# Cross-attention and a scanned state space on one Trainium2 core: scores and value products on quarters of the TensorE array, one shared PSUM bank fewer, and the end of the kernel as planned pieces

## The chip, the core and the metric

The kernel runs on one core of one Trainium2 chip. The metric is device time in microseconds (us) of one execution. Before the change three runs took 2513.02, 2515.10 and 2516.12 us; the median is 2515.1 us. One more execution was profiled; it took 2515.3 us, of which 2513.5 us lie between the first and the last instruction (the span).

## The reference, cut to what matters

There is one batch entry, 4096 query rows of width 512, 3202 context rows, 8 heads of width 64, and everything is float32.

```python
x = _layernorm(builder_state, g1, beta1)
base_n = _layernorm(base_state, g1, beta1)
x = residual + _mha(x, base_n, W_qkv, b_qkv, W_o, b_o)   # softmax(q k^T / 8) v, then W_o
xn = _layernorm(x, g2, beta2)
U = (xn @ W_in.T + b_in) @ Bmat                          # 4096 x 64
def step(s, u_t):
    s = jax.nn.silu(s @ A.T) + u_t
    return (s, s)
_, states = jax.lax.scan(step, 0, U)                     # 4096 steps, one after another
x = residual + states @ Cmat
mod = program_probs.mean(axis=1) @ W_prog.T + b_prog
return x + mod
```

The attention is the large part: 4096 x 3202 scores for each of 8 heads, the exponential of each, and the product of the weights with the values. The scan is sequential, but its state is forgotten quickly, so the kernel runs it in many stretches at once and checks whether the start of each stretch agrees with the end of the one before.

## The kernel before, in words

**Preparation** (the first 258 us of the profile). The context is normalized, turned and multiplied with the weights; keys and values are written to device memory (`kd`, `vd`). Small matrices of the scan are made beside it.

**The loop over steps.** The queries are cut into 8 blocks of 512 rows. A *unit* is one block, one pair of heads (`hp`, two heads of 64 make 128 partitions) and one half of the block (256 queries, `QU`). There are 64 units. A unit goes through the keys in 13 *steps*; a step takes two groups of 122 to 124 keys (`b` is 0 or 1) for both heads of the pair (`a` is 0 or 1). So there are 832 steps, and each of them does this:

- `scores` (L605, TensorE): four matmuls, one for each `b` and `a`. The 64 rows of one head contract, so each uses half of the rows of the array, and the 123 keys are its output partitions. The result `s` is [keys, a, b, 256] and fills two PSUM banks, one for each head.
- `keep` (L618, ScalarE) copies `s` to SBUF as `p`; `running` (L633, VectorE) keeps the running maximum over the steps in `top`.
- After the 13th step the maximum over keys is taken across partitions: `spread` (TensorE transposes, tile `tt`), `maximum` (VectorE), `everywhere` (TensorE, tile `mb`).
- `subtract` (L664, VectorE) and `weights` (L674, ScalarE, the exponential) work on `p` in place.
- `product` (L691, TensorE): four matmuls, one for each `b` and `a`. All 123 keys contract, and the 64 value columns of a head are half of the columns of the array. They accumulate over the 13 steps in one bank, `po`.
- `add` (L682, GpSimd) sums the weights over the steps into `acc`; this is the denominator.

The float32 matmul of one call appears in the profile as two weight loads and two matmuls, so both `scores` and `product` have 8 records of each kind in a step.

At the end of a unit, `output` (L737) copies `po` to SBUF, `both`, `turn`, `inverse`, `wide` and `back` turn the denominator into a factor, and `scale` applies it. Once in a block, the rows are projected (`outs`, L900), normalized, and turned into inputs of the scan (`inputs`, `kept`); the queries of the next block are normalized and projected beside it (`heads`, L294).

**PSUM** has 8 banks. The loop gives 4 to `s` (two buffers of two banks), 1 to `mb`, 1 to `po`, and 2 to a pool `ps_m`, from which every other piece of TensorE work takes its bank: `spread`, `turn`, `back`, the transposes of queries and rows, `heads`, `outs`, `inputs`.

**The order.** The order of the instructions on each engine is written out by hand through a planner (`Plan`, L54). Every piece has an engine, a cost, the pieces that it follows, a due time (step number times `STEP`, shifted by `SHIFT` for its sort) and the buffers that it takes and gives back. `order` (L92) lists the pieces by a simulated clock: when an engine is free, it takes the ready piece with the earliest due time whose buffers fit. For scores and products it adds 200 ns (`START`) when the kind of TensorE work changes and 65 (`AGAIN`) when it stays, and prefers runs of two of one kind (`RUN`). On the chip each engine then runs its list strictly in that order. The transfers are issued by SyncE from the same lists: `load_k` in the score pieces and `load_v` in the score or product pieces.

**The last unit and the end.** For the last unit six of the 13 partial denominators are made by TensorE with a matrix of ones (`PE_SUMS`, L708) instead of GpSimd. When the planner's pieces are through, `main_scan` (L1136) and `last_rows` (L1175) run as two Python generators that are advanced in turn. The scan makes two sweeps of 16 steps over all stretches (`sweep`, L1062): sweep a from zero, sweep b from the ends that sweep a found. A scan step is a matmul (L1072), a tanh on ScalarE (L1085) and a product on VectorE (L1086). Sweep a also issues bfloat16 matmuls on zeros (L1078). In sweep b, each step adds `states` (GpSimd), `products` (L1102, TensorE) and `outputs` (additions on VectorE, ScalarE and GpSimd, and two stores). `last_rows` takes the last 256 rows through projection, normalization and 24 short scan steps of their own (L1250). A comparison of ends and starts (`differ`) closes the kernel, and a correcting loop follows it that runs only where they differ.

## Time and profile before

| What | us |
|---|---|
| median of three runs | 2515.1 |
| the profiled execution, and its span | 2515.3, 2513.5 |
| preparation, to the first score matmul | 257.9 |
| scores of the first unit, to the first product | 257.9 to 295.7 |
| loop, first product to last score | 295.7 to 2398.4 |
| last products and denominators | to 2436.6 |
| sweep a and the last rows | 2436.6 to 2462.5 |
| sweep b with the outputs, and the short scan | 2462.5 to 2502 |
| last outputs, comparison, end | 2502 to 2513.5 |

| In 600 to 2100 us | busy us of 1500 |
|---|---|
| PE (TensorE matmul) | 1480.17 |
| POOL (GpSimd) | 1414.12 |
| DVE (VectorE) | 1391.14 |
| ACT (ScalarE) | 1289.17 |

In these 1500 us some 580 steps pass, 2.59 us each. The columns of a group row are: line, engine, operation, output and inputs, shapes, count, then busy time in us and the mean ns of one, then the idle time of the engine just before them and what ended it. PEld is the loading of weights, which runs beside the matmuls. Busy time counts an overlap once.

### The profile page before, as it was taken

Reading aid. Unit: us, or ns where it says so; the run is one execution under the profiler, and the core shown is the slowest. Engines: PE = TensorE matmul, PEld = TensorE weight load, DVE = VectorE, ACT = ScalarE, POOL = GpSimd, SP = SyncE. Lnnn points to the kernel's source line nnn. Section 1 sums busy time; section 2 is a strip of 40 time slices with the busy share of each in tenths; the row PEclk is TensorE's granted clock in tenths of the full one; section 3 lists DMA queues with packets and bytes.
Section 4 is the critical chain, followed back from the end, with each engine's and each line's share of the span. In section 5 each row is a group of like instructions: output and inputs, shape, how many; then the busy total and the mean of one; then the engine's idle time right before and its main releaser. Section 6 shows DMA issues by size and latency. Waiting matters only on the chain.

```text
span 2513.5 us, 43994 instructions
## 1 busy us (share of the span) xinstructions
PE 2418.6 (96%) x16390; PEld 1409.1 (56%) x16392; DVE 2087.6 (83%) x2242; ACT 1922.3 (76%) x2373; POOL 2066.7 (82%) x1195
## 2 busy tenths in 40 slices
PE   7999899999999999999999999999999999999987
PEld 3444555655565555655565556555565556555543
DVE  2220699999999989899999999999989899999964
ACT  2222588878987898788987898789878888888852
POOL 1110299989998999899998999899989999899963
PEclk9999999999999999999999999999999999999998
DMA  3422322112211222122211221222212221233364
GB/s 120 131 99 79 88 64 62 45 48 68 66 56 53 66 66 66 49 62 85 64 49 43 68 78 46 60 67 67 58 48 67 74 64 53 83 115 118 107 165 144
DMA packets 178035, 189.21 MB, mean 75 GB/s; under 512 B 14252, under 2 KB 151256, under 8 KB 177818
## 3 DMA queue, kind: packets, MB, share of 16 engines
q1 hardware_dynamic: 173270, 178.67, 23.7%
q10 hardware_dynamic: 4548, 7.67, 1.0%
q8 instruction: 133, 2.18, 0.4%
q14 instruction: 84, 0.69, 0.1%
HBM read 156.40 MB, written 29.89 MB: 74 GB/s over the span
## 4 chain that ended last, share of the span: by engine, by line
PE 38%; DVE 22%; POOL 17%; issue 13%; ACT 6%; DMA 2%; SPq 1%; ACTq 0%; POOLq 0%; DVEq 0%
POOL acc L682 15%; DVE top L633 12%; PE s L605 12%; PE po L691 9%; DVE p L664 6%; ACT p L618 3%; PE pv L534 3%; PE pk L560 3%; PE pq L294 3%; PE pa L900 2%; ACT p L674 2%; PE tt L641 1%; POOL both L747 1%; PE pd L753 1%; DMA cx<-in_ctx_dram 1%
## 5 line engine op out<-in xcount | busy, mean ns | idle before, releaser
L682 POOL TENSOR_TENSOR acc<-p,acc 122x1024 f32<-122x1024 f32 (+1 forms) x698 | 1653.0, 2368 | 60.7 <-ACT p L674 17.9
L664 DVE TENSOR_TENSOR p<-p,mb 123x1024 f32<-123x1024 f32 (+2 forms) x832 | 991.7, 1208 | 23.2 <-PE mb L656 23.2
L674 ACT ACTIVATE p<-p 123x1024 f32<-123x1024 f32 (+2 forms) x832 | 875.4, 1058 | 138.9 <-DVE p L664 134.2
L618 ACT COPY p<-s 123x1024 f32<-123x1024 f32 (+2 forms) x832 | 829.6, 1006 | 168.4 <-PE s L605 121.6
L605 PE MATMUL s<-q,k 64*123 64x256 f32 (+2 forms) x6656 | 911.1, 398 | 25.2 <-DVE top L633 15.0
L691 PE MATMUL po<-p,v 123*64 123x256 f32 (+2 forms) x6656 | 877.5, 390 | 6.6 <-ACT p L674 4.7
L633 DVE TENSOR_TENSOR top<-s,top 123x1024 f32<-123x1024 f32 (+1 forms) x640 | 777.3, 1215 | 11.5 <-ACT p L618 9.3
L605 PEld LDWEIGHTS s<-q,k 64*123 64x123 f32 (+2 forms) x6656 | 574.9, 182 | 337.7 <-DVE top L633 115.9
L691 PEld LDWEIGHTS po<-p,v 123*64 123x64 f32 (+2 forms) x6656 | 423.5, 136 | 357.9 <-issue 145.5
L682 POOL TENSOR_TENSOR acc<-p,p 124x1024 f32<-124x1024 f32 x64 | 152.3, 2380 | 121.2 <-DMA k<-kd 73.8
L633 DVE TENSOR_TENSOR top<-s,p 124x1024 f32<-124x1024 f32 x64 | 78.2, 1222 | 99.3 <-ACT p L618 66.3
L294 PE MATMUL pq<-xn,wq 128*128 128x256 f32 x512 | 126.7, 390 | 0.0
L243 POOL TENSOR_SCALAR ve_c<-mv_c 123x1 f32<-123x1 f32 (+2 forms) x26 | 6.1, 233 | 145.7 <-DVE mv_c L236 117.8
L900 PE MATMUL pa<-wo,o 128*128 128x512 f32 x240 | 116.9, 609 | 0.0
L504 DVE COPY ct<-tp_c 128x492 f32<-128x492 f32 (+2 forms) x13 | 8.7, 672 | 123.3 <-PE tp_c L270 123.3
L294 PEld LDWEIGHTS pq<-xn,wq 128*128 128x128 f32 x512 | 92.2, 189 | 31.6 <-issue 21.2
L568 ACT ACTIVATE ks<-pk,bias 128x492 f32<-128x492 f32 (+3 forms) x28 | 18.0, 643 | 118.6 <-PE pk L560 58.4
L534 PE MATMUL pv<-wv,ct 128*123 128x512 f32 (+2 forms) x208 | 99.0, 621 | 0.0
L560 PE MATMUL pk<-ct,wk 128*128 128x492 f32 (+3 forms) x224 | 89.1, 550 | 0.0
L747 POOL TENSOR_TENSOR both<-acc 124x512 f32<-124x512 f32 x63 | 80.8, 1283 | 3.0
L648 DVE TENSOR_REDUCE m<-tt 128x4 f32<-128x496 f32 x64 | 42.9, 671 | 42.7 <-PE tt L641 42.7
L534 PEld LDWEIGHTS pv<-wv,ct 128*123 128x123 f32 (+2 forms) x208 | 39.1, 196 | 46.0 <-issue 45.1
(196 smaller groups left out, 1486.3 us busy)
## 6 DMA issues: line engine op xcount, KB each, us to landing
k<-kd SPq DMA_DIRECT2D x324, 123.0 KB
v<-vd SPq DMA_DIRECT2D x324, 123.0 KB
k<-kd SPq DMA_DIRECT2D x108, 124.0 KB
v<-vd SPq DMA_DIRECT2D x108, 124.0 KB
xr<-in_x_dram SPq DMA_DIRECT2D x32, 256.0 KB
x1d<-xr SPq DMA_DIRECT2D x32, 256.0 KB
x<-in_x_dram SPq DMA_DIRECT2D x28, 256.0 KB
cx<-in_ctx_dram SPq DMA_DIRECT2D x18, 246.0 KB
```

What stands on the lines that cost most here:

```text
L294: nc.tensor.matmul(pq[:, half * QU : (half + 1) * QU], wq[:, i, hp * P : (hp + 1) * P], xns[half][:, i, :], start=(i == 0), stop=(i == NC ...
L534: nc.tensor.matmul(pv[:n, :H], ct[:, i, o : o + n], wv[:, i, :], start=(i == 0), stop=(i == NC - 1),)
L560: nc.tensor.matmul(pk[:, :n_g], wk[:, i, hp * P : (hp + 1) * P], ct[:, i, :n_g], start=(i == 0), stop=(i == NC - 1),)
L605: nc.tensor.matmul(s[:n, a, b, :], kts[(*w["at"][:2], c)][r, b * n : (b + 1) * n], q[r], start=True, stop=True,)
L618: nc.scalar.copy(t[:n], w["ps"][c][:n])
L633: nc.vector.tensor_tensor(w["top"][:n], s[:n], before[:n], ALU.max)
L664: nc.vector.tensor_tensor(t[:n], t[:n], w["mb"][:n].unsqueeze(2).to_broadcast([n, 2, 2, QU]), ALU.subtract,)
L674: nc.scalar.activation(t[:n], t[:n], AF.Exp)
L682: nc.gpsimd.tensor_tensor(w["acc"][:n], t[:n], before[:n], ALU.add)
L691: nc.tensor.matmul(w["po"][a * HD : (a + 1) * HD, 0, :], vts[(*w["at"][:2], c)][:n, b, a * HD : (a + 1) * HD], t[:n, a, b, :], start=(c == ...
L747: nc.gpsimd.tensor_tensor(w["both"], acc[:, :, 0, :], acc[:, :, 1, :], ALU.add)
L900: nc.tensor.matmul(v["pa"], o_t[Q, c, t // 2][:, t % 2 * P : (t % 2 + 1) * P], wo[:, c, :], start=(c == 0), stop=(c == NC - 1),)
```

## The change

Five things change.

1. `scores` makes eight matmuls in a step: the keys of a group are cut at 64, so that each matmul uses 64 rows and at most 64 columns of the array. The output goes to the upper or the lower half of the partitions of the same two banks.
2. `product` makes eight matmuls in a step: the keys that contract are cut at 64 too. The two key halves accumulate in two banks of a wider `po`. `output` copies the first, and a new VectorE operation for each unit, `join`, adds the second.
3. The second bank of `po` comes from `ps_m`, which has one bank in the loop instead of two. In the preparation a second pool `ps_n` keeps two.
4. The planner counts 10 ns for a change between scores and products and 200 after other work, runs are of one, and the table `SHIFT` is new.
5. The end of the kernel becomes pieces of the plan. Sweep a may start as soon as the last scores have left their banks, beside the last unit's products; the matmuls on zeros are gone. Sweep b starts when sweep a has ended, and the last rows start when the last unit is through. `products` is issued in two halves of 256 columns. In the last unit TensorE makes three of the partial denominators instead of six, GpSimd nine.

```diff
-    START, AGAIN = 200, 65
-    RUN = 2
-    ALONE = dict(scores=600, product=2600)
+    START, AGAIN = 200, 10
+    RUN = 1
+    ALONE = dict(scores=300, product=1300)
...
-                    cost += (self.AGAIN if same else self.START) if p["kind"] else 0
+                    cost += (self.AGAIN if last else self.START) if p["kind"] else 0
...
-    ps_m = actx.enter_context(tc.tile_pool(name="ps_m", bufs=2, space=PSUM))
+    ps_m = actx.enter_context(tc.tile_pool(name="ps_m", bufs=1, space=PSUM))
+    m_pools = [ps_m]
+
+    def m_tile(shape, name):
+        pool = m_pools.pop(0)
+        m_pools.append(pool)
+        return pool.tile(shape, F32, tag="m", name=name)
...
+    m_pools.append(prep.enter_context(tc.tile_pool(name="ps_n", bufs=1, space=PSUM)))
...
+    m_pools[:] = [ps_m]
     prep.close()
...
         for b in range(2):
-            for a in range(2):
-                r = slice(a * HD, (a + 1) * HD)
-                nc.tensor.matmul(
-                    s[:n, a, b, :],
-                    kts[(*w["at"][:2], c)][r, b * n : (b + 1) * n],
-                    q[r],
-                    start=True,
-                    stop=True,
-                )
+            for k0, k1 in ((0, HD), (HD, n)):
+                for a in range(2):
+                    r = slice(a * HD, (a + 1) * HD)
+                    nc.tensor.matmul(
+                        s[k0:k1, a, b, :],
+                        kts[(*w["at"][:2], c)][r, b * n + k0 : b * n + k1],
+                        q[r],
+                        start=True,
+                        stop=True,
+                        skip_group_check=True,
+                    )
...
-            w["po"] = ps_o.tile([P, 2, QU], F32, tag="o", name=f"po_{w['name']}")
+            w["po"] = ps_o.tile([P, 2, 2 * QU], F32, tag="o", name=f"po_{w['name']}")
         for b in range(2):
             for a in range(2):
-                nc.tensor.matmul(
-                    w["po"][a * HD : (a + 1) * HD, 0, :],
-                    vts[(*w["at"][:2], c)][:n, b, a * HD : (a + 1) * HD],
-                    t[:n, a, b, :],
-                    start=(c == 0 and b == 0),
-                    stop=(c == NDC - 1 and b == 1),
-                )
+                for k, (k0, k1) in enumerate(((0, HD), (HD, n))):
+                    nc.tensor.matmul(
+                        w["po"][a * HD : (a + 1) * HD, k, :QU],
+                        vts[(*w["at"][:2], c)][k0:k1, b, a * HD : (a + 1) * HD],
+                        t[k0:k1, a, b, :],
+                        start=(c == 0 and b == 0),
+                        stop=(c == NDC - 1 and b == 1),
+                        skip_group_check=True,
+                    )
...
+    def join(w):
+        o = o_t[w["at"]]
+        nc.vector.tensor_tensor(o, o, w["po"][:, 1, :QU], ALU.add)
...
-    PE_SUMS = range(2, NDC, 2)
+    PE_SUMS = (4, 8, 12)
+    A_PACE, B_PACE = 1500, 1900
...
-            elif fill:
-                for _ in range(fill):
-                    nc.tensor.matmul(
-                        sv["fill"], zeros[:, :P], zeros, start=True, stop=True
-                    )
...
-    def products(j, s):
+    def products(j, s, part=slice(0, H)):
         for v, n in enumerate(counts):
             r = slice(v * NS, (v + 1) * NS)
-            nc.tensor.matmul(sv["py"][j % 2][v], s[r, :], sv["c2"][r], start=True, stop=True)
+            nc.tensor.matmul(
+                sv["py"][j % 2][v][:, part], s[r, :], sv["c2"][r, part], start=True, stop=True,
+                skip_group_check=True,
+            )
...
+            plan.add(("join", i), "DVE", 400, partial(join, w), [("output", i)], d + 500, [],
+                     [("o", ("product", i, 0))])
...
+        plan.add("start", "DVE", 600, ready_scan, ["fetch"] + kept_, d + 2 * STEP, ["s", "s"])
...
+        for p in sweep("a", None, "end1", d + 3 * STEP, A_PACE, ["start"]):
+            plan.add(*p)
+
+        d += 16 * STEP
+        last_unit(plan, ws[n], n, d)
+        last_rows(plan, d)
+        for p in sweep("b", "end1", "end0", d + STEP, B_PACE, [("a", "end")]):
+            plan.add(*p)
...
+                plan.add(("products", j, part), "PE", 590, partial(products_, j, part),
+                         [("states", j), *free[j % 2]], e + 1000 + part)
...
-                s=2, m=2, b=1, o=1, p=NDC + LAG + 4, top=2, acc=2, both=1, q=6, x=3, x1=2, xn2=1,
+                s=2, m=1, b=1, o=1, p=NDC + LAG + 4, top=2, acc=2, both=1, q=6, x=3, x1=2, xn2=1,
...
-        for _ in last_rows(ws[len(units) - 1]):
-            next(scan, None)
-        for _ in scan:
-            pass
-        last_outputs("a")
-        differ(sv["sl"][:, : P : LT], sv["st"], P // LT, sv["badl"])
```

## The prediction

> **What bounds the kernel now.** I begin with the page's first two parts: busy time by engine, and the span in 40 slices.
>
> ```profile
> PE 2418.6 (96%) x16390; PEld 1409.1 (56%) x16392; DVE 2087.6 (83%) x2242; ACT 1922.3 (76%) x2373; POOL 2066.7 (82%) x1195
> ...
> PE   7999899999999999999999999999999999999987
> ...
> DVE  2220699999999989899999999999989899999964
> ACT  2222588878987898788987898789878888888852
> POOL 1110299989998999899998999899989999899963
> ```
>
> In the loop (slices 6 to 38) three engines stand at 9, so relief for one alone may buy little. The second view is the same in microseconds for a stretch of the loop, and for the end. Its columns are: length, then PE, PEld, DVE, ACT and POOL busy (instructions), the granted TensorE clock, the DMA share, GB/s.
>
> ```profile
> 600.00:2100.00 1500.00, 1480.17 (x10749) 884.04 (x10750) 1391.14 (x1400) 1289.17 (x1570) 1414.12 (x765) 1.00 0.21 62
> 2436.60:2462.50 25.90, 21.23 (x102) 11.94 (x102) 10.58 (x30) 7.07 (x22) 4.58 (x8) 1.00 0.45 116
> 2462.50:2498.00 35.50, 32.13 (x140) 15.57 (x140) 22.22 (x67) 13.02 (x45) 19.83 (x27) 0.99 0.61 205
> ```
>
> PE works 98.7% of the loop and its clock is full, so it sets the pace: 2.59 us for a step. How near the others are behind it is seen in their waits. Third view, waits on VectorE and GpSimd from 298 to 2403 us: in total, times, longest.
>
> ```profile
> POOL acc L682 <- ACT p L674: 63.9, 44, 5.6
> ...
> DVE top L633 <- ACT p L618: 66.8, 59, 2.4
> DVE m L648 <- PE tt L641: 41.9, 37, 2.0
> DVE p L664 <- PE mb L656: 17.0, 14, 1.7
> DVE s L627 <- ACT p L618: 8.8, 11, 1.7
> ```
>
> GpSimd waits 63.9 of 2105 us, 3.0%, though it is busy only 94%: the rest lies between its instructions. In the timeline five additions in a row take 12.19 us, and one takes 2.37 (row L682), so they start 12.19 less 2.37, over 4, or 2.45 us apart; 0.08 us of each is a gap that nobody ends. GpSimd without waits would need 2.59 x 0.970 = 2.51 us for a step. VectorE waits 135.9 us with a small fifth row, 6.5%, so its floor is 2.42. **The loop is bound by PE, and 0.08 us behind it stands GpSimd, which the change doesn't relieve.**
>
> Fourth view, PE's timeline (start, length from first start to last end, line, operation, count):
>
> ```profile
> 1301.29 1.99 PE L605 MATMUL s<-q,k 64*123 64x256 f32 x16
> 1303.21 1.08 PE L691 MATMUL po<-p,v 123*64 123x256 f32 x8
> ...
> 1305.81 1.13 PE L605 MATMUL s<-q,k 64*123 64x256 f32 x8
> 1306.87 1.08 PE L691 MATMUL po<-p,v 124*64 124x256 f32 x8
> 1307.89 0.44 PE L771 MATMUL rb<-ident,wide 128*128 128x128 f32 x2
> ```
>
> By the starts, scores alone hold PE 1.06 us (1305.81 to 1306.87) and products 1.02. Two score steps in a row hold it 1.92, so the second costs only 0.86. A change of kind thus costs 0.20 before scores and 0.16 before products; without one, eight matmuls in pairs take four slots of 0.216 us.
>
> **The change, part by part. Quarters.** The streamed columns stay: a step's scores become 16 matmul records instead of 8, and if four run at once instead of two they again take four slots, 0.86 us. What can go is the price of changing kind. The row cannot tell whether scores and products in quarter form count as one kind. Here the Trainium skill helps (TensorEngine Tiling (Array Packing), Key Properties): a change of tiling mode drains the array, a change of tile within a mode doesn't, and both would now be 64 x 64. So I take 0.86 for either. Had each kept its change, a step would hold 1.06 + 1.02 as now.
>
> Can it be issued so fast? Twice as many records in the same time are 16 loads and 16 matmuls in 0.86 us. The densest row that is sustained are the one-column matmuls of the preparation:
>
> ```profile
> 116.94 0.54 PEld L438 LDWEIGHTS pb<-bi,bm 128*64 128x64 f32 x8 [0.16 <-issue]
> 116.94 0.63 PE L438 MATMUL pb<-bi,bm 128*64 128x1 f32 x8
> 117.40 0.55 PEld L442 LDWEIGHTS pb<-be2s,wcr 128*64 128x64 f32 x8
> ```
>
> Eight loads with eight matmuls start in 0.46 us (116.94 to 117.40), 58 ns for a pair, on one tile, where each matmul also waits for its own load. Sixteen would be 0.92 us. A rule speaks against even that: TensorE: Matmul & The Clock Gate, Part 1, puts the sequencer at some 62 ns for each matmul when hardware decode is off, 0.99 us for sixteen. The row is under it, so it decides. Lower end 0.86 (slots), upper end 0.92; I take 0.87, since loads of different tiles overlap in L605, where a pair of tiles starts as one.
>
> A second rule speaks against it more strongly: the same page, Part 3, says a weight load overlaps a running matmul only in other rows of the array. By it each quarter slot would add a load of 0.136 us (mean of the L691 loads): 4 x 0.352 = 1.41 us, and the step below would come to 3.50. But L691 uses all rows, has eight such loads, and still holds PE 1.02 us. I keep the row.
>
> PE's other work, from the groups of the trace (busy time of L294 126.7, L900 116.9, L656 42.4, L641 40.6, L753 40.4, L948 32.6, L771 27.6 and 40.4 of L270 for queries and rows), is 467.6 us over 832 steps, 0.56 a step. About 7.5 such pieces in a unit of 13 steps (four of its own, 28 in a block of eight units) each still force a change back, 0.20, so 0.12 a step. PE after: 2 x 0.87 + 0.56 + 0.12 = 2.42 us (2.52 at the upper end). That is no longer the bound; GpSimd at 2.51 is. VectorE gets one `join` for a unit, near the 0.41 us of L779, which has the same size: 0.03 a step, 2.45. It lies in VectorE's waits; if there were none, it would cost 64 x 0.41 = 26 us.
>
> So at most GpSimd's 63.9 us can go. Three engines between 2.42 and 2.51 in strict order won't run without waits; I take half of it, **32 us** (a step of 2.55). Ends: nothing and 64.
>
> **One bank for everything else.** Its users in a unit are `tt`, `pd` and `rb`, and in a block 20 more, so 44 in 104 steps, 352 in all. PE waits with all that is behind it (scores and products, and so ScalarE, VectorE and GpSimd) when the reader of the bank before is late. PE's slack against today's pace is 2.59 - 2.42 = 0.17 us a step, 138 us in all, or 0.39 us for each user. I put the cost at nothing within the 32: the planner counts the bank as taken, and other matmuls stand between users.
>
> **First unit.** 13 score steps run with little beside them; each loses its change of kind, 0.20 us: **3 us**.
>
> **The end.** Sweep a moves beside the last unit's products, and with it 15 of the L1072 matmul pairs, tanhs and products; no transfer moves with it. From 2436.6 on, PE is busy 21.2 of 25.9 us, then 32.1 of 35.5, so the end is mostly PE work too, and moving it saves only what it idles (4.7 + 3.4, and 2.7 between 2403 and 2436.6: 10.8 us) and what is left out: the matmuls on zeros (L1078, 7.3 us) and three sums at 0.86 (2.6). Against it: 16 scan matmuls between products are changes of kind, 16 x 0.16 = 2.6. At best 10.8 + 7.3 + 2.6 - 2.6 = 18 us. In the list of the changed kernel the sweep's matmuls stand between the last unit's products, and sweep b begins before the last product, so half of the idle time should go: 18 - 5 = 13, less 3 for GpSimd's three added partial sums (7.3 us of additions that lie beside VectorE's 13 subtractions for the most part). **10 us.** Ends: -10 (each scan step waits in three queues behind pieces of 0.9 to 1.2 us) and 18.
>
> Sum: the profiled execution's span is 2513.5, its time 2515.3; 2515.3 - 32 - 3 - 10 = 2470.3. It lies 0.2 over the median of the runs shown, so **2470 us**.
>
> **The rivals.**
> *B, GpSimd holds the loop where it is.* If its waits come from unit boundaries (44 of them, all on weights, about one for a unit), a faster PE need not shorten them: the chain from last score to maximum to first weight runs through VectorE and ScalarE. For it: VectorE's waits for `tt` too. Against: that chain contains scores and transposes that queue behind PE. Only first unit and end are won: 2502. The change then doesn't do what it says in the loop.
> *C, waits vanish.* GpSimd becomes the only bound, buffers fill, and boundaries are bridged: 2515 - 64 - 3 - 18 = 2430.
> *D, slower: the single bank stalls PE.* Place: any second user of `ps_m` at the head of PE's list. It decides from 0.39 us for each of 352 users, plus what the end wins (13 / 352 = 0.04). A full VectorE operation of 1.2 us that has to pass before the reader, half of the time, is 0.6: 352 x (0.6 - 0.43) = 60, so 2575.
> *E, slower: quarters don't run four at a time at full pace.* From 0.955 us for eight (2 x 0.955 + 0.68 = 2.59) the loop is slower; at 1.08 (a slot of 0.27, one 0.055 us load exposed) a step is 2.84, 0.25 x 813 = 203 more: some 2700.
>
> **How the numbers follow.** Mine 0.45, B 0.23, C 0.13, D 0.12, E 0.07. Mine spans 2450 to 2490. The time is mine, 2470. The range leaves out D and E at the top and the lowest of C: 2422 to 2514. Faster or slower by 0.2% (5 us) is about what a measurement tells from no change. Mine, C and 0.20 of B are faster, 0.78; 0.04 is same; slower is 0.18.
>
> **What would show it.** Sixteen matmuls of L616 starting within 0.86 to 0.93 us, and a product after scores at that distance too: right on the quarters. GpSimd's waits under 40 us and PE near 94% in the loop: right on the bound. PE idle before scores, ended by a reader of `ps_m`: D. Scan steps with a distance of over 2.5 us beside the last unit: the end is dearer. Were GpSimd's additions themselves to change from 2.37 us, my floor would be wrong in either direction.

## The result, and the profile after it

The changed kernel takes 2486.5 us (median of four runs, 2485.2 to 2487.9), the kernel before it 2515.2 (median of four beside it, 2513.0 to 2516.1). The ratio is 0.989, with a 95% interval of 0.9876 to 0.990. The prediction was 2470 us with a range of 2422 to 2514: the direction and the range held, and the point was 16.5 us too low.

The profiled execution's span fell from 2513.5 to 2483.4 us, by 30.1. First come the page's busy times and slices of the changed kernel.

```profile
PE 2296.9 (92%) x29718; PEld 1355.7 (55%) x29718; DVE 2108.2 (85%) x2307; ACT 1917.3 (77%) x2373; POOL 2071.5 (83%) x1197
...
PE   7999888999999999999999999999998999999987
...
DVE  2111599999999999999999999999999999999975
ACT  2223588888987899788988988789978998888852
POOL 1111199989998999989998999899999999899984
```

TensorE has nearly twice the records and 121.7 us less busy time. VectorE and GpSimd have nearly the same work as before (VectorE 20.6 us more, with 64 `join` operations of 0.41 us in it). The span fell by only a quarter of what TensorE lost. Next, the same stretch of the loop as before, and the two parts of the end: from the last score to the last product, and from there to the end. The columns are length; busy time of PE, PEld, DVE, ACT and POOL; the granted TensorE clock, the DMA share, GB/s. First the kernel before, for the end only, then the changed one.

```profile
2398.40:2434.50 36.10, 32.19 (x212) 17.28 (x210) 23.69 (x30) 19.39 (x21) 30.36 (x15) 0.91 0.67 177
2434.50:2513.50 79.00, 59.75 (x274) 30.90 (x272) 38.03 (x117) 21.01 (x71) 25.47 (x35) 0.90 0.49 152
```

```profile
600.00:2100.00 1500.00, 1419.59 (x20232) 864.54 (x20224) 1422.35 (x1463) 1301.43 (x1588) 1431.93 (x773) 1.00 0.22 64
2373.20:2422.30 49.10, 43.35 (x398) 22.05 (x392) 31.14 (x52) 23.26 (x38) 39.94 (x20) 0.97 0.73 192
2422.30:2483.40 61.10, 44.33 (x256) 27.77 (x248) 33.05 (x99) 16.32 (x54) 24.88 (x34) 0.84 0.44 149
```

In the loop TensorE now works 94.6%, VectorE 94.8% and GpSimd 95.5% of the time: three engines stand within one per cent of each other. At the end the last unit became longer (36.1 to 49.1 us) and what follows it shorter (79.0 to 61.1), together 4.9 us less.

Placed on the time axis, the 30.1 us are: 1.5 us more until the first score (257.9 and 259.4), 0.7 less in the first unit (34.3 and 33.5 from its first score to its first subtraction), 25.9 less in the loop (2106.2 and 2080.3 from there to the last score), and 4.9 less at the end.

The waits of VectorE and GpSimd, in the changed kernel from 298 to 2370 us (in total, times, longest):

```profile
DVE m L660 <- PE tt L653: 57.6, 35, 3.9
...
POOL acc L694 <- ACT p L686: 46.7, 54, 2.8
...
ACT p L630 <- POOL acc L694: 24.4, 28, 2.2
...
DVE p L676 <- PE mb L668: 22.2, 24, 1.6
...
DVE top L645 <- ACT p L630: 8.0, 26, 0.9
```

GpSimd's waits for weights fell from 63.9 to 46.7 us, VectorE's wait for scores that are kept (L645, before L633) from 66.8 to 8.0; its wait for the transposes of the maximum (`tt`) rose from 41.9 to 57.6. Last, TensorE's timeline of the changed kernel at the place that the prediction showed (start, length from first start to last end, line, operation, count):

```profile
1301.80 1.09 PE L705 MATMUL po<-p,v 64*64 64x256 f32 x16
1302.72 1.05 PE L616 MATMUL s<-q,k 64*64 64x256 f32 x16
1303.58 1.05 PE L705 MATMUL po<-p,v 64*64 64x256 f32 x16
...
1307.62 1.93 PE L705 MATMUL po<-p,v 64*64 64x256 f32 x32
1309.35 1.07 PE L616 MATMUL s<-q,k 64*64 64x256 f32 x16
```

Scores that follow products hold TensorE 0.86 us (1302.72 to 1303.58), and two products in a row 1.73 (1307.62 to 1309.35). The counts are records, two for each matmul. So the sixteen records of a step's quarters take the time that eight records of halves took without a change of kind, and between scores and products that price is gone.

### The profile page after: what moved, and what is told of

It reads as the page before. It is cut to its first block, busy times and chain, and to the rows that moved or that the text cites. A ratio compares the mean times of both kernels' runs of the same rounds, so it can differ in the third digit from the quotient of the medians.

```text
span 2483.4 us, 70816 instructions
## 1 busy us (share of the span) xinstructions
PE 2296.9 (92%) x29718; PEld 1355.7 (55%) x29718; DVE 2108.2 (85%) x2307; ACT 1917.3 (77%) x2373; POOL 2071.5 (83%) x1197
## 3 DMA queue, kind: packets, MB, share of 16 engines
q8 instruction: 237, 3.88, 0.7%
## 4 chain that ended last, share of the span: by engine, by line
PE 44%; DVE 21%; POOL 13%; issue 10%; ACT 8%; DMA 2%; SPq 1%; ACTq 0%; POOLq 0%; DVEq 0%
PE s L616 13%; PE po L705 12%; POOL acc L694 12%; DVE top L645 12%; DVE p L676 6%; PE pq L302 5%; ACT p L630 4%; ACT p L686 3%; PE pv L543 3%; PE pk L569 3%; PE pa L902 1%; PE mb L668 1%; PE tt L653 1%; PE pd L755 1%; DMA x<-in_x_dram 1%
## 5 line engine op out<-in xcount | busy, mean ns | idle before, releaser
L694 POOL TENSOR_TENSOR acc<-p,acc 122x1024 f32<-122x1024 f32 x701 | 1660.3, 2369 | 64.1 <-ACT p L686 26.2
L616 PE MATMUL s<-q,k 64*64 64x256 f32 (+3 forms) x13312 | 884.9, 384 | 90.9 <-DVE top L645 79.9
L705 PE MATMUL po<-p,v 64*64 64x256 f32 (+3 forms) x13312 | 857.3, 379 | 26.9 <-ACT p L686 25.1
L645 DVE TENSOR_TENSOR top<-s,top 123x1024 f32<-123x1024 f32 (+1 forms) x640 | 777.4, 1215 | 11.8 <-ACT p L630 11.3
L616 PEld LDWEIGHTS s<-q,k 64*64 64x64 f32 (+3 forms) x13312 | 448.2, 130 | 428.6 <-DVE top L645 154.5
L705 PEld LDWEIGHTS po<-p,v 64*64 64x64 f32 (+3 forms) x13312 | 489.8, 133 | 268.4 <-ACT p L686 70.0
L302 PEld LDWEIGHTS pq<-xn,wq 128*128 128x128 f32 x512 | 92.2, 189 | 34.3 <-issue 23.6
L645 DVE TENSOR_TENSOR top<-s,p 124x1024 f32<-124x1024 f32 x64 | 78.0, 1219 | 37.8 <-DMA k<-kd 31.8
L902 PEld LDWEIGHTS pa<-wo,o 128*128 128x128 f32 x240 | 40.6, 189 | 51.9 <-issue 50.8
```

Of the source, the lines that this page charges most:

```text
L302: nc.tensor.matmul(pq[:, half * QU : (half + 1) * QU], wq[:, i, hp * P : (hp + 1) * P], xns[half][:, i, :], start=(i == 0), stop=(i == NC ...
L616: nc.tensor.matmul(s[k0:k1, a, b, :], kts[(*w["at"][:2], c)][r, b * n + k0 : b * n + k1], q[r], start=True, stop=True, skip_group_check=True,)
L645: nc.vector.tensor_tensor(w["top"][:n], s[:n], before[:n], ALU.max)
L694: nc.gpsimd.tensor_tensor(w["acc"][:n], t[:n], before[:n], ALU.add)
L705: nc.tensor.matmul(w["po"][a * HD : (a + 1) * HD, k, :QU], vts[(*w["at"][:2], c)][k0:k1, b, a * HD : (a + 1) * HD], t[k0:k1, a, b, :], sta ...
L902: nc.tensor.matmul(v["pa"], o_t[Q, c, t // 2][:, t % 2 * P : (t % 2 + 1) * P], wo[:, c, :], start=(c == 0), stop=(c == NC - 1),)
```

## A view that the averages hide

From the second query block to the seventh the loop repeats itself every eight units (one block), to 0.3 us. The units of such a block are unlike each other, because the projections of queries (the heads) and of outputs fall into a few of them. So I cut one block into its units, each from its first subtraction to that of the next. These are the windows of the changed kernel for the units 16 to 23.

```profile
819.20:851.66 32.46, 30.52 (x434) 17.97 (x426) 31.89 (x35) 28.42 (x35) 31.51 (x19) 1.00 0.31 88
851.66:883.16 31.50, 30.08 (x443) 18.07 (x442) 30.66 (x33) 27.72 (x37) 30.79 (x18) 1.00 0.18 55
883.16:919.60 36.44, 34.90 (x485) 21.19 (x484) 33.12 (x34) 33.98 (x47) 35.31 (x25) 1.00 0.28 86
919.60:952.38 32.78, 30.78 (x425) 17.48 (x427) 30.91 (x33) 29.54 (x41) 31.97 (x22) 1.00 0.18 59
952.38:985.35 32.97, 30.03 (x474) 18.43 (x478) 32.44 (x33) 30.23 (x38) 32.02 (x17) 1.00 0.27 72
985.35:1020.52 35.17, 35.17 (x434) 22.86 (x430) 31.21 (x33) 27.49 (x31) 34.23 (x16) 1.00 0.11 31
1020.52:1052.73 32.21, 32.17 (x498) 21.53 (x494) 30.35 (x32) 26.03 (x29) 31.02 (x15) 1.00 0.24 65
1052.73:1085.48 32.75, 27.99 (x438) 15.53 (x438) 32.34 (x33) 26.90 (x30) 26.88 (x12) 1.00 0.16 48
```

Read the largest of PE (second number), DVE (fourth) and POOL (sixth) in each line against the length. The length is that largest number plus 0 to 1.1 us, and the engine that has it changes: VectorE in the 1st, 5th and 8th unit, GpSimd in the 2nd, 3rd and 4th, TensorE in the 6th and 7th. In the 6th, which has three heads, TensorE has no idle time at all (35.17 of 35.17); in the 8th it idles 4.8 us. The second engine stands only 0.1 to 1.2 us behind the largest in the first seven. The largest number says which engine has least room, not yet which one holds the unit; e6 and e11 below show the difference. The kernel before, for the same block:

```profile
822.50:854.07 31.57, 31.09 (x219) 17.78 (x220) 30.43 (x32) 27.59 (x34) 29.96 (x18) 1.00 0.23 69
854.07:890.85 36.78, 36.35 (x266) 21.61 (x266) 32.80 (x34) 31.91 (x43) 35.82 (x22) 1.00 0.21 65
890.85:924.86 34.01, 32.95 (x242) 20.04 (x242) 31.56 (x33) 30.79 (x42) 32.89 (x22) 1.00 0.28 85
924.86:956.99 32.13, 31.84 (x226) 18.03 (x224) 30.43 (x33) 29.97 (x41) 31.17 (x21) 1.00 0.15 47
956.99:991.98 34.99, 34.44 (x270) 20.14 (x270) 32.20 (x32) 30.58 (x37) 33.96 (x18) 1.00 0.26 72
991.98:1026.05 34.07, 33.80 (x232) 22.02 (x230) 31.06 (x32) 26.51 (x29) 32.97 (x16) 1.00 0.11 34
1026.05:1061.18 35.13, 34.96 (x256) 21.72 (x254) 31.16 (x33) 28.31 (x31) 32.66 (x15) 1.00 0.21 62
1061.18:1092.53 31.35, 31.09 (x240) 17.79 (x238) 30.93 (x32) 25.32 (x28) 24.37 (x11) 1.00 0.17 54
```

There TensorE has the largest number in all eight units, in the third by only 0.06. I use two sums over the eight units from here on: the largest of the three engines in each unit, added up ("the largest work"), and the rest of the block's length ("the waits").

| kernel | block of 8 units | largest work | waits | TensorE / VectorE / GpSimd busy |
|---|---|---|---|---|
| before | 270.0 | 266.5 | 3.5 | 266.5 / 250.6 / 253.8 |
| changed | 266.3 | 262.1 | 4.2 | 251.7 / 252.9 / 253.7 |

TensorE lost 14.9 us in a block, and the block 3.7. The other 11 us became TensorE's idle time. The wait that grew is that of the scores for VectorE's running maximum, which must have read a score tile before its two banks may be filled again (first the kernel before, 298 to 2403 us, then the changed one, 298 to 2370 us):

```profile
PE s L605 <- DVE top L633: 13.5, 46, 0.7
```

```profile
PE s L616 <- DVE top L645: 76.0, 130, 1.4
```

A TensorE that is done sooner waits at the score tiles. There are two of them; with a third, for which no bank was free, nothing was tried.

## The experiments

Theory 1 (T1 in the expectations) is the prediction's account: quarters make TensorE faster, GpSimd is the next bound, half of its waits is what can be won, and the one bank costs nothing. Theories 2 to 4 came up on the way and are told where they did. Differences in us are taken from the changed kernel's 2486.5, if nothing else is said, and ratios are to the kernel before, which ran beside each group (its medians there were 2512.7 to 2516.1).

**Halves again, in the new order (e1_halves).** `join` takes a maximum of the same two values, so that VectorE's work stays.

```
-            for k0, k1 in ((0, HD), (HD, n)):
+            for k0, k1 in ((0, n),):
...
-                for k, (k0, k1) in enumerate(((0, HD), (HD, n))):
+                for k, (k0, k1) in enumerate(((0, n),)):
...
-        nc.vector.tensor_tensor(o, o, w["po"][:, 1, :QU], ALU.add)
+        nc.vector.tensor_tensor(o, o, w["po"][:, 0, :QU], ALU.max)
```

> The changed kernel with scores and products on halves of the array again, as before the change (four matmuls of 123 columns or rows instead of eight of 64 or 59), everything else and the order of the list kept; join becomes a maximum of the sum with itself, so that VectorE's work stays. Theory 1 (the loop's gain is the price of changing kind, 0.20 and 0.16 us, which quarters do without, up to where GpSimd and VectorE bound): PE needs 1.06 + 1.02 + 0.56 + 0.12 = 2.76 us a step at most, some 2.66 with a few runs of one kind: 80 us more than the changed kernel, about 2565, and slower than the kernel before. Rival (the new order and the new end brought the gain, the quarters nothing): 2486, within 8 us.

Measured: 2571.5 us (2568.8 to 2575.4), ratio 1.023 (1.0216 to 1.025). In its timeline the price of the changes is back, 1.06 and 1.02 us:

```profile
1305.56 1.13 PE L616 MATMUL s<-q,k 64*123 64x256 f32 x8
1306.62 1.08 PE L705 MATMUL po<-p,v 123*64 123x256 f32 x8
1307.64 1.13 PE L616 MATMUL s<-q,k 64*123 64x256 f32 x8
```

TensorE's busy time in a block is 268.7 us instead of 251.7, or 0.163 a step, which is the 0.17 of the prediction. In this order the quarters are worth 85 us, three times what the whole change gives. The order must therefore be costly without them. The run shows that the quarters remove the price of changing kind; it doesn't show what the array does during a change.

**The planner's table of before (e2_old_table).** Quarters, one bank and the new end stay; `START, AGAIN`, `RUN`, `ALONE`, `SHIFT` and the test in `cost` go back.

```
-    START, AGAIN = 200, 10
+    START, AGAIN = 200, 65
-    RUN = 1
+    RUN = 2
-    ALONE = dict(scores=300, product=1300)
+    ALONE = dict(scores=600, product=2600)
...
-        "back": -2600, "both": -1300, "everywhere": -2600, "heads": 2000, "heads2": -5800,
-        "maximum": 18900, "output": -1300, "product": 1300, "query.copy": -300,
-        "query.spread": -3200, "query.turn": 1200, "row.inputs": -1300, "row.mean": 2000,
-        "row.mod": 8100, "row.row": 6500, "row.spread": -1300, "row.turn": 2300, "row.x1": 2600,
-        "scores": -300, "spread": 600, "turn": -1900, "weights": 1300,
+        "back": -2600, "both": -1300, "everywhere": -2600, "heads": 2000, "heads2": -5200,
+        "maximum": 18900, "output": -5200, "product": 1300, "query.spread": -5800,
+        "query.turn": 1200, "row.mean": 2000, "row.mod": 7800, "row.row": 1300, "row.spread": -600,
+        "row.turn": 2600, "spread": -2000, "turn": -1900, "weights": 1300,
...
-                    cost += (self.AGAIN if last else self.START) if p["kind"] else 0
+                    cost += (self.AGAIN if same else self.START) if p["kind"] else 0
```

> The changed kernel with the planner's numbers of before: START 200 and AGAIN 65 for the same kind, runs of two, ALONE and the whole table SHIFT of before; quarters, one bank and the new end stay. Theory 1: quarters need no runs of a kind and the loop is near GpSimd's floor, so the order is worth little: 2486 to 2500. Rival (the table is what lets the loop live with one bank and faster PE): 2515 or more.

Measured: 2536.2 us (2532.1 to 2537.7), ratio 1.009 (1.0073 to 1.0107). With the old table the change is slower than the kernel it came from, and the new table is worth 50 us, which I had given no share of its own. In the block of units 16 to 23 the largest work is 263.5 us, near the changed kernel's 262.1; the waits are 9.3 instead of 4.2 (11.0 in the block of units 32 to 39). TensorE's own busy time is 5 us higher too; I didn't trace why.

**The kernel before with one bank (e7_before_one_bank).** Halves and the old table; the second bank of `ps_m` is held and not used by the loop.

```
-    ps_m = actx.enter_context(tc.tile_pool(name="ps_m", bufs=2, space=PSUM))
+    ps_m = actx.enter_context(tc.tile_pool(name="ps_m", bufs=1, space=PSUM))
...
-                s=2, m=2, b=1, o=1, p=NDC + LAG + 4, top=2, acc=2, both=1, q=6, x=3, x1=2, xn2=1,
+                s=2, m=1, b=1, o=1, p=NDC + LAG + 4, top=2, acc=2, both=1, q=6, x=3, x1=2, xn2=1,
```

> The kernel before with one bank instead of two for everything else in the loop (m = 1 in the plan; the freed bank stays empty until the last rows), halves and all else as before; the planner lists the pieces anew for one bank. Theory 1 as in the prediction: the planner counts the bank as taken, so it costs nothing to speak of: 2513 to 2525. Rival D (a second user at the head of PE's list waits for the reader of the first, 0.5 us for most of 352 users): 2560 or more.

Measured: 2537.4 us (2532.9 to 2538.3), ratio 1.008 (1.0064 to 1.0097). Under the old table the one bank costs 22 us, 2.5 in a block (272.6 for 270.0; 1.5 of it largest work and 1.1 waits). That is less than rival D priced, and more than my nothing. It ends within 2 us of e2_old_table: under the old table, with one bank, quarters and the new end win nothing together, and under the new table quarters alone win 85. The parts don't add: what a faster TensorE is worth depends on the list.

**GpSimd relieved (e3_skip_add).** The addition of step 6 is left out, 2.4 us in a unit, so the sums that the weights are divided by lack one step.

```
-        nc.gpsimd.tensor_tensor(w["acc"][:n], t[:n], before[:n], ALU.add)
+        if c != 6:
+            nc.gpsimd.tensor_tensor(w["acc"][:n], t[:n], before[:n], ALU.add)
```

> The changed kernel without GpSimd's addition of step 6 in each unit, so that the denominator lacks that step; all other instructions and their order stay. GpSimd loses 2.45 us of a unit, 0.19 of a step. Theory 1 (GpSimd is the loop's bound, its floor 2.50 of 2.555 us): the step falls until VectorE's floor of 2.445 or its waits hold it, 40 to 80 us less: 2410 to 2445. Rival (VectorE paces the loop, since scores wait for its maximum): 2480 to 2487.

Measured: 2482.5 us (2481.8 to 2485.8), ratio 0.987 (0.9857 to 0.989): 4.0 us less, where GpSimd is busy 151 less. Its work went over into waits (298 to 2370 us):

```profile
POOL acc L695 <- ACT p L686: 130.9, 82, 4.5
```

46.7 us became 130.9. **So GpSimd doesn't set the loop's pace, and theory 1 falls in this step.** It follows, at almost full load.

**VectorE relieved (e4_skip_top).** The running maxima of steps 5 and 8 are left out (2.0 us of VectorE's busy time in a unit), so the maximum that is subtracted lacks two steps.

```
-        nc.vector.tensor_tensor(w["top"][:n], s[:n], before[:n], ALU.max)
+        if c not in (5, 8):
+            nc.vector.tensor_tensor(w["top"][:n], s[:n], before[:n], ALU.max)
```

> The changed kernel without VectorE's running maximum of steps 5 and 8 in each unit, so that the maximum subtracted misses these two steps; all other instructions and their order stay. VectorE loses 2 x 1.13 us of a unit, 0.17 of a step, and two score buffers come free earlier. Theory 1 (GpSimd bounds): at most GpSimd's remaining waits of 47 us can go, about 15: 2470 to 2486. Rival (VectorE paces the loop): 60 to 120 us less, at most down to GpSimd's floor, which then is 2440: 2440 to 2460.

Measured: 2475.1 us (2474.8 to 2479.8), ratio 0.985 (0.9834 to 0.9867): 11.5 us less for 129 us of VectorE's busy time. That lies in the range that theory 1 gave, which e3 has ruled out, and above the 2440 to 2460 of VectorE as the pace setter.

**TensorE relieved by a whole step (e5_skip_product).** By now theory 2 was that no engine alone is the bound. The products of step 6 are left out.

```
-            product(w, c)
+            if c != 6:
+                product(w, c)
```

> The changed kernel without the products of step 6 in each unit (the output lacks the values of that step; their transfers stay). PE loses 0.86 us of a unit, 0.066 of a step, 54 in all. Theory 2, made after the relief of GpSimd gave 4 us and that of VectorE 11.5 (no engine alone bounds; each has a floor of 2.42 to 2.50 us a step, and the strict order with two score buffers loses some of every engine's wait): 5 to 20 us less, 2467 to 2482. Rival (PE still paces the loop, its busy 94.6% is what counts): 40 to 54 less, 2432 to 2447.

Measured: 2541.9 us (2541.2 to 2542.2), ratio 1.010 (1.0087 to 1.012). It is slower with less work, so it says nothing on TensorE's share. The row that stands out is the copy that keeps the scores and waits for a GpSimd addition to release its tile:

```profile
ACT p L630 <- POOL acc L694: 90.4, 50, 7.1
```

That wait is 24.4 us in the changed kernel, longest 2.2. Without the product the tile's last reader is another engine, so tiles may be handed on in another order; that is argued and not shown. It taught me to leave every tile its last reader in e9 below.

**Both relieved (e6_skip_both).** The cuts of e3 and e4 together.

> The changed kernel without GpSimd's addition of step 6 and without VectorE's maximum of steps 5 and 8 (denominator and maximum lack these). Theory 2: with GpSimd at 2.31 and VectorE at 2.27 us a step as floors, the loop should fall by more than the sum of the two single reliefs (15.5 us), to PE's floor of 2.42 with waits: 2430 to 2455. Rival (neither is at the bound at all; PE or the chain at the change of units is): about the sum, 2468 to 2474.

Measured: 2456.1 us (2455.1 to 2457.2), ratio 0.976 (0.9746 to 0.9779): 30.4 us less, twice the 15.5 of the two alone, and 1 us above the range that theory 2 gave. Two of its units, the third of the block and the sixth:

```profile
873.75:910.20 36.45, 34.91 (x485) 21.14 (x484) 31.07 (x33) 34.08 (x48) 32.83 (x25) 1.00 0.27 84
975.55:1010.72 35.17, 35.17 (x434) 22.87 (x430) 29.30 (x31) 27.45 (x31) 32.77 (x15) 1.00 0.10 31
```

They are as long as in the changed kernel (36.44 and 35.17), though VectorE and GpSimd have 1.5 to 2.5 us less in them. In the sixth TensorE leaves no room. In the third GpSimd had the largest number in the changed kernel, and 2.5 us less of it changed nothing. The gain came from other units. This gave theory 3: the bound changes from unit to unit.

**TensorE relieved, with all readers in place (e9_half_products).** In four steps only one of the two key chunks is multiplied. By the profile TensorE is busy 90 us less in all, 1.4 in a unit; the 110 of the expectation were too many.

```
-        for b in range(2):
+        for b in range(1 if c in (3, 5, 7, 9) else 2):
```

> This kernel leaves out half of the value products (the second key chunk of the pair) in steps 3, 5, 7 and 9 of each unit; every tile is still read by the same last piece, so no buffer changes hands at another place. TensorE has 4 x 0.43 = 1.7 us less in each unit of 13 steps, 110 us in all; VectorE, ScalarE and GpSimd keep their work. Theory 3, the bound changes from unit to unit (in a block of eight, TensorE has no idle time in the units with the heads and little in the one with two output projections, and VectorE or GpSimd is behind it elsewhere): only these three of eight fall, by 1.2 to 1.7 us each, 24 units: 2445 to 2458 us. If TensorE paced all units: 2385 to 2420. If it paced none, as the prediction's floor has it: 2478 to 2487.

Measured: 2478.3 us (2472.5 to 2480.2), ratio 0.987 (0.9852 to 0.9885): 8.3 us less for 90 us of TensorE's busy time, where theory 3 expected 29 to 41. The time lies where the expectation put a TensorE that paces nothing. The interval overlaps that of the changed kernel; in the traces the loop is 7.6 us shorter. The same two units:

```profile
880.79:916.70 35.91, 33.54 (x453) 19.82 (x452) 33.03 (x34) 33.76 (x46) 34.78 (x25) 1.00 0.29 87
983.92:1017.80 33.88, 33.88 (x410) 21.96 (x406) 31.21 (x34) 27.39 (x31) 33.02 (x15) 1.00 0.10 32
```

The second fell by 1.29, as theory 3 says. The first fell by 0.53 and is 1.1 us above GpSimd, which is at 34.78 there. TensorE's wait for VectorE's maximum, 76.0 us in the changed kernel, is 118.1 here (298 to 2370 us). (The expectation gives this unit two output projections; the changed kernel's trace has one in it, and also sixteen matmuls of `pu`, fifteen transposes of L270 and fourteen products.) So "which engine is largest" isn't enough, since the others stand so close behind it. That is theory 4.

**The heads spread over the block (e10_spread_heads).** Nothing is left out; each head waits for a score step 9 steps after that of the head before.

```
-        head_pieces(plan, Q, range(NC), xns, copied, d, QSTEP // 2,
+        head_pieces(plan, Q, range(NC), xns, copied, d - 6 * STEP, 9 * STEP,
...
-            plan.add(("heads", Q, hp), "PE", 1850, head, copied, d, ["m", "q"], xn_)
+            plan.add(("heads", Q, hp), "PE", 1850, head, copied + [from_(d)] if Q else copied, d, ["m", "q"], xn_)
```

> The same work as the changed kernel, with the same number of pieces; only the query heads (3.84 us of TensorE each, four in a block of eight units) are held back so that they start in four units instead of three in one and one in the next. Theory 3: the unit that has three heads, 35.2 us and no idle TensorE, falls to 32 to 33, the unit that has none and idles TensorE for 4.8 us rises by at most 0.5, so 2 to 3 us for a block, seven blocks: 2463 to 2475 us. If an average slack of TensorE over the whole loop counted, the place of the heads would not matter: 2483 to 2490.

Measured: 2485.9 us (2483.8 to 2490.1), ratio 0.989 (0.9876 to 0.9909): no change, as if the place of the heads didn't matter. But the largest work of the block of units 16 to 23 did fall, from 262.1 to 260.5 us, and the waits rose from 4.2 to 7.0. (The first unit of this block has a mean clock of 0.95; the block of units 32 to 39 has 260.3 and 5.6.) The first seven blocks together are 1.6 us shorter than in the changed kernel, and the stretch from there to the last score is 4.0 longer. Moving the heads moved other pieces in the list too:

```profile
852.09:886.05 33.96, 31.01 (x436) 17.98 (x435) 31.89 (x35) 29.41 (x39) 32.92 (x22) 1.00 0.21 70
886.05:920.07 34.02, 34.02 (x481) 20.66 (x480) 31.80 (x35) 31.70 (x44) 32.98 (x21) 1.00 0.26 81
...
985.58:1020.95 35.37, 34.51 (x466) 21.66 (x466) 32.34 (x34) 28.65 (x32) 34.43 (x16) 1.00 0.15 45
```

The third unit fell by 2.4 us, the one ahead of it rose by 2.5, and the sixth, which has two heads now by the order of TensorE's list, stayed at 35.4. Here a more even load didn't pay; whether it would with a list made for it was not tried.

**All three relieved (e11_all_three).** The cuts of e3, e4 and e9 together.

> The cuts of three kernels together: no GpSimd addition of step 6, no VectorE maximum of steps 5 and 8, and no second half of the products of steps 3, 5, 7 and 9. Alone they took 4, 11 and 8 us from the time, the first two together 30. Theory 4 (all three engines stand within 1 to 3 us of saturation in every unit, so relief shows only where all that are near get it): TensorE, which idles under 2.4 us in six of eight units once the other two are relieved, now gives back most of its 1.7 us a unit: 2456 - 48 x 1.0 to 1.5, so 2385 to 2410 us. If single reliefs only add (something else, the order's chain of waits, holds the units): 2456 - 8, so 2444 to 2452.

Measured: 2428.6 us (2426.7 to 2432.2), ratio 0.966 (0.9643 to 0.9673): 57.9 us less, where the three alone gave 4.0 + 11.5 + 8.3 = 23.8. Halving the products, worth 8.3 us alone, is worth 27.5 once the other two have less to do. So theory 4 holds in kind: the three engines cover each other. In size it expected 46 to 71 for the last step. The third unit, at 35.65 us, still stands 2.1 above TensorE and 2.8 above GpSimd; ScalarE, which was never relieved, is at 33.62 in it, as high as TensorE (33.55). The block shows where the rest went: the largest work fell by 12.9 us, from 262.1 to 249.2, but the waits rose from 4.2 to 9.8, and the block is 258.9. GpSimd's waits for weights are at twice those of the changed kernel (298 to 2340 us):

```profile
POOL acc L696 <- ACT p L687: 97.9, 79, 3.5
```

The list is written for the planner's costs, which weren't changed; why just these waits grow is open.

| left out | busy less in all: TensorE / VectorE / GpSimd | gain, medians | gain, the loop in the traces |
|---|---|---|---|
| an addition (e3) | 1 / 1 / 151 | 4.0 | 2.6 |
| half of four products (e9) | 90 / 1 / 2 | 8.3 | 7.6 |
| two maxima (e4) | 6 / 129 / 2 | 11.5 | 10.1 |
| addition and maxima (e6) | 12 / 132 / 150 | 30.4 | 30.2 |
| all (e11) | 100 / 133 / 151 | 57.9 | 57.8 |

**Sweep a behind the last product (e8_sweep_a_late).** The end undone in this one part.

```
-        for p in sweep("a", None, "end1", d + 3 * STEP, A_PACE, ["start"]):
+        for p in sweep("a", None, "end1", d + 16 * STEP, A_PACE, ["start", ("product", n, NDC - 1)]):
```

> The changed kernel with sweep a after the last unit's last product instead of beside the products; the rest of the end as changed. As predicted, with the move worth what PE idles: 8 to 12 us more, about 2496. Rival (the 49 us that the last unit takes from last score to last product, where it was 36, eat what the move wins, and the gain of the end is the missing matmuls on zeros and sums alone): 2483 to 2489.

Measured: 2505.4 us (2498.6 to 2509.3), ratio 0.996 (0.9944 to 0.9978). That is 19 us more. In its profile the last unit takes 32.6 us from last score to last product, and 90.9 follow. So the sweep costs the last unit 16.5 us (49.1 less 32.6) and takes 29.8 from what follows (90.9 less 61.1), 13.3 in all; the last score, too, comes 3.8 later there, 2.8 of them before the loop, where the edit changes nothing. And it isn't the move alone that is priced. For 20.5 us of the late sweep the granted clock is half:

```profile
2416.49:2436.97 20.48, 15.05 (x36) 7.38 (x34) 6.87 (x17) 2.76 (x8) 3.99 (x8) 0.50 0.23 66
```

In the kernel before, whose late sweep has the matmuls on zeros in it, the clock is 1.00 throughout (2436.6 to 2462.5 us, in the prediction's second view). Four records of the last rows' projection (L1193) take 3.78 us in e8 at half clock and 1.98 in the changed kernel. From the last score to the end e8 takes 123.5 us and the kernel before 115.1, though e8 leaves out the zeros; the half clock is the one cause that I saw. A late sweep with the zeros was not run.

**The last rows' projection later (e12_rows_late).** In the timeline of the changed kernel two pieces stand between the last unit's maximum and its spreading to all partitions:

```profile
2380.18 1.09 PE L705 MATMUL po<-p,v 64*64 64x256 f32 x16 [1.52 <-ACT p L686]
2381.20 3.62 PE L1193 MATMUL py<-wo,o 128*128 128x512 f32 x4
2384.62 0.70 PE L668 MATMUL mb<-ident,m 128*124 128x128 f32 x4
```

```
-                     ["start", ("scale", i)] + ([("last", c - 1)] if c else []), d + (2 + 2 * c) * STEP)
+                     ["start", ("scale", i)] + ([("last", c - 1)] if c else []), d + (5 + 3 * c) * STEP)
```

> The same work as the changed kernel; only the projection of the last rows (L1193) is due later, so that no piece of it stands ahead of the transposes of the last unit's maximum on TensorE, where one of 3.55 us stands now. If TensorE's list holds the last unit: the first subtraction of that unit starts 3 us earlier and the end with it, 2481 to 2485 us. If the scan beside it or the later place of the projection holds the end: 2485 to 2490.

Measured: 2482.1 us (2477.1 to 2492.7, five runs), ratio 0.988 (0.9863 to 0.9896). The timeline of this kernel has only the first scan matmul there:

```profile
2380.74 0.91 PE L1060 MATMUL z<-u,a_t 128*128 128x384 f32 x2
2381.49 0.60 PE L668 MATMUL mb<-ident,m 128*124 128x128 f32 x4
```

`mb` starts 3.1 us earlier, as expected, and the median is 4.4 us lower. Part of the 3.1 us is clock and not order: in the changed kernel L1193 runs at a mean clock of 0.53 there (2381.2 to 2384.8 us), and four such records take only 1.88 us at 1.00 a little later (2387.10). The intervals of the two kernels overlap, though, and they did not run beside each other: this is the lowest median of a kernel that leaves nothing out, and not shown to be better.

## Why the prediction was right or wrong

- **Quarters at full pace: right.** The eight matmuls of a step's scores, or of its products, hold TensorE 0.86 us (0.87 taken), and TensorE is busy 0.946 of a step of 2.56, 2.42 us (2.42 predicted). The drain that the prediction leaned on agrees: no price between two uses of 64 x 64, and it is back in e1. The two rules that were weighed against the rows didn't apply: sixteen matmul records in 0.86 us are 54 ns each, below the sequencer's 62, and no weight load is exposed (sixteen of 0.133 us pass in the same 0.86), though the Trainium skill (TensorE: Matmul & The Clock Gate, Part 3) lets loads overlap only in other rows. Rival E is out.
- **"That is no longer the bound; GpSimd at 2.51 is": wrong.** This is the step that failed. It set one average over the loop against another. GpSimd relieved by 151 us gave 4 (e3), VectorE by 129 gave 11.5 (e4), TensorE by 90 gave 8.3 (e9), all three 57.9 (e11). No one floor is next; the units' loads differ, in each of them two or three engines stand close together, and of the 89 us of idle time that TensorE gained in the loop (37.0 and 126.2), 62 are the wait for VectorE's maximum (13.5 us before, 76.0 after).
- **"I take half of it, 32 us": near in size, by a reason that doesn't hold.** The loop gave 25.9. GpSimd's waits fell only by 17.2. The half was a guess, and that it came near is luck. The blocks say where the gain is: TensorE's 14.9 us less in a block lowers the largest work by only 4.4, since VectorE or GpSimd has the largest number in six of eight units, and the waits take 0.7 back. The second to the seventh block gave 3.6 to 3.9 each, 22.5 in all, the first block 0.4, and the stretch from the eighth block's first subtraction to the last score 3.0.
- **One bank at nothing within the 32: held, but not for the reason given.** TensorE's slack didn't hide it in general: under the old table, with halves, the one bank costs 22 us (e7). In the changed kernel the waits of TensorE that a reader of `ps_m` ends are 3.2 us or less in each row, and the new table is worth 50 us (e2). The prediction gave the table no term. Rival D's price was too high by more than half, and its mechanism isn't seen: in e7, too, the waits that a reader of `ps_m` ends for a user that doesn't need its data are 2.3 us or less in each row. The 22 us then lie in the list that the planner makes for one bank; that is argued.
- **First unit, 3 us: wrong, 0.7.** In it the scores stand in ones and twos between query heads, so the change of kind to and from a head stays, and two score steps in a row had no change before either (1.92 for two, 1.89 now). There was little to win.
- **The end, 10 us: half, 4.9.** The term that failed is "half of the idle time should go" (5.4 of 10.8). From the last score to the end TensorE's idle time fell by only 0.7 us (23.2 to 22.5), its busy time by 4.3 (91.9 to 87.7; the terms 7.3 + 2.6 - 2.6 make 7.3). The last unit had 3.9 us of idle time to fill and was given 11.2 us more work (32.2 to 43.4), so it grew by 13.0. A scan matmul between two products holds 0.42 us there (2397.29 to 2397.71 in the timeline), and the product behind it pays for the change of kind, 1.02 for 0.86. The 7.3 us for the matmuls on zeros can't be taken alone either: a late sweep without them runs at half clock for 20.5 us (e8), while beside the products, from 2384.8 us on, the clock is 1.00 without them.
- **The sum.** 30.1 instead of 45: the loop 6.1 short, the end 5.1, the first unit 2.3, and 1.5 more before the first score. These 1.5 are within what differs from run to run: in the traces of the eleven other kernels built from the changed one the first score comes at 257.4 to 262.3 us.
- **Rivals.** B (loop unchanged) and C (waits vanish) both stand against a loop that gave 25.9: TensorE's relief was worth something, and the waits stayed, 46.7 us for GpSimd where under 40 was to show my case. PE near 94% in the loop came true (94.6) and so was no sign of GpSimd as the bound.

## What to carry to other kernels

When the bound is relieved and two other engines are within 5% of it, don't put the gain at the distance to the next average. Cut the loop into its repeating units, take the largest engine in each, and add these up: that gave 4.4 us a block here for a relief of 14.9. This sum was read after the change. From the eight rows of before alone, with the 14.9 us taken evenly from TensorE, it would have been 5.3, or some 42 for eight blocks (an estimate), where 26 came and the prediction said 32. So the sum shows where the limit lies; it did not forecast the size better. Then expect single experiments to show little; relieve engines in pairs before calling any of them harmless. And a list written by a planner is itself a term in the sum: the table was worth 50 us here, where the whole change gave 29.

## What the runs showed of the hardware that was not expected

Sixteen matmul records with sixteen weight loads on four quarters of the array take 0.86 us, one such group after the other without loss, closer than the densest row of the kernel before (58 ns for a pair of load and matmul, here 54). The instruction queue moves 3.88 MB instead of 2.18, for 70,816 instructions instead of 43,994, and no wait that I read points to it.

The granted clock of TensorE isn't a constant at the end. Over the last 61 us of the changed kernel it is 0.84 in the mean, where the kernel before has 0.90 over its last 79, but that is no slower work throughout: it is 1.00 up to 2463.3 us, and half in the last 20, where TensorE is busy 7 us.

```profile
2463.30:2483.40 20.10, 7.35 (x26) 4.28 (x25) 8.46 (x33) 1.77 (x8) 1.27 (x1) 0.50 0.24 82
```

The kernel before has 0.50 in its last 16.4 us, with TensorE busy 4.3. In e8 the same happens in the middle of the sweep and costs time there. In the five runs of e12_rows_late the span follows the mean clock: 2475.2 us at 0.995, 2479.9 and 2480.3 at 0.992, 2481.6 at 0.991, 2490.9 at 0.988. Only the first of them was traced, so which stretch lost its clock in the others, and whether that is the cause of their length or goes with it, is open. The spread of a kernel's runs is here as large as the gains looked for at the end.
